# A window attention's scores and softmax weights turned and spread by DMA through DRAM

## The chip, the cores and the metric

The kernel runs on one core of one Trainium2 chip. The metric is the device time of one execution, in microseconds (us), as the median of several runs. Every engine and row below belongs to that one core.

## What is computed

A decoder of four layers over 16 sequences of 64 x 512 numbers in float32. Each layer is a cross attention followed by a feed-forward block, each with a residual. The layers are of different kinds. The change touches only the attention of the first one (layer 0), and the second layer's attention matters because its work is interleaved with it. Cut to these two:

```python
# layer 0: 64 channels, 8 heads of 8 channels, T = 512 positions, windows of 16
q = Wq @ x + bq; k = Wk @ cond + bk; v = Wv @ cond + bv      # (B, 64, 512)
k, v = pad(k, 8 left, 7 right), pad(v, 8 left, 7 right)
dots[b,h,t,w] = sum_d q[b,h,d,t] * k[b,h,d,t+w] * 8**-0.5
attn = softmax(dots, over w)                                  # 16 numbers each
out[b,h,d,t] = sum_w attn[b,h,t,w] * v[b,h,d,t+w]
x = x + Wo @ out + bo
# layer 0: an int8-quantised gated feed-forward block
# layer 1: attention with 32 query and 8 key heads of 128, RMS-normed q and k,
#          over the context's 64 rows and the latents' 64 rows
s = q @ k.T * 128**-0.5; p = softmax(s); x = x + (p @ v) @ Wo
```

So layer 0 needs, for each head and position, 16 scores, each a sum over 8 channels, and 16 weights, each of which is the same for 8 channels.

## The kernel before

**Tiles.** The activations are eight tiles x of 128 x 512 (two sequences of 64 channels each), and stay in SBUF from the first layer to the last. Layer 0 takes them in four groups of two tiles.

**Two lanes and a written order.** The program of TensorE is written out by hand: two lanes are Python generators that record instructions and yield a cost after each step, and `merged(main, side)` (line 1369) advances the side lane by the costs that the main lane has yielded, times a rate. The side lane (`first_layers`, then more) computes layer 0 for one group after another: window attention, then the int8 feed-forward block. The main lane computes layer 1's attention (`normed_attention`) for the groups that layer 0 has finished. It first makes the context's keys (line 679) and then runs its units of queries (722), keys and values (740), scores (543), softmax, turned weights (137), values (583) and output projection (592). A `Need(n, rate)` makes the main lane wait for layer 0's mark n and sets the rate from there on: 1.1 at the start, then 0.88, 0.8, 0.8 and 0.72 for the groups. After the fourth group's mark the second half of the network follows. Only TensorE's order is fixed by hand; a tile scheduler orders the other engines. Each lane has four of the eight PSUM banks.

**Layer 0's attention for a group of two tiles** (`WindowAttention`; P is 128, NH = 32 is the number of heads of two tiles, which are four sequences, and NG = 4 windows are handled at once):

1. `inputs` (lines 255 to 270): TensorE makes q, k and v, ScalarE copies them out with their bias into qs, kp and vp, the last two padded.
2. Scores: for each of four groups g of four windows and for each of the two tiles, VectorE multiplies qs with four shifted views of kp (line 293, two instructions of 128 x 1024 elements into a tile of products), and TensorE sums over the 8 channels of a head by a product with a 0/1 matrix `group` (line 300). ScalarE copies the sums into dots (line 308). There a row is a pair of window and head, and a column is a position.
3. Turn: the softmax runs over windows, which lie on partitions. In four chunks of 128 positions TensorE transposes the four blocks of dots (line 316), so that a row is a position and the 16 windows lie along a row.
4. Softmax per chunk: maximum over the windows on VectorE (324), subtraction (325), exponential on ScalarE (326), sum (328), reciprocal (329), multiplication on GpSimd (330).
5. Turn back: TensorE transposes e (the helper at line 137, result `ps_att`), ScalarE copies it into att (338).
6. Output, for each tile and each group g of four windows (`output`): four products with a 0/1 matrix `spread` (line 367) copy each head's weight to its 8 channels, one PSUM bank for each window. VectorE multiplies each bank with a shifted view of vp (377, 128 x 512). GpSimd adds the four windows: line 379 with 128 x 1024 elements, then two additions of 128 x 512 (383, or 385 and 386). At the end TensorE multiplies the sum with Wo (356, `ps_o`), and VectorE adds it to x (395). In the first group of tiles each of the four sums is multiplied with Wo by itself (n_sums is 4); in the others a single sum over all windows is (n_sums is 1).

The tiles of products have two buffers, which the scores' prod and the output's pv share; cn (the context's rows) and e share three row buffers.

**DMA.** All transfers are issued by SyncE, in program order of the scheduler. Layer 1's weights, a store of the context's keys and values (line 701) and their loads as kT and v (lines 714 to 719) go that way, too. Layer 0 uses DMA only for x, the context and its weights.

Of the kernel before, what the change touches and what calls it, by code (L numbers as in the profile page):

```python
# [8 lines left out]
F32 = mybir.dt.float32  # L9
# [4 lines left out]
AF = mybir.ActivationFunctionType  # L14
ALU = mybir.AluOpType
AX = mybir.AxisListType

P = 128
B, S, D = 16, 64, 512
NTOK = B * S  # L20
NT = NTOK // P
NC = D // P
# [7 lines left out]
def bc(ap, axis, n):  # L30

    a = ap.unsqueeze(axis)
    shape = list(a.shape)
    shape[axis] = n
    return a.to_broadcast(shape)
# [162 lines left out]
class WindowAttention:  # L198
# [6 lines left out]
    def __init__(self, es, ln, ctx_in, wt, bias):  # L205
        self.ln, self.ctx_in = ln, ctx_in
        k, nc = ln.k, ln.nc
        NH = self.NH
        pool = ln.pool(es, "l0c", 1)

        self.group = pool.tile([P, 2, NH], F32, tag="group", name="group")
        nc.gpsimd.memset(self.group, 0.0)

        self.spread = pool.tile([P, 2 * P], F32, tag="spread", name="spread")
        for i in range(2):
            nc.vector.tensor_reduce(
                self.group[:, i, 16 * i : 16 * (i + 1)],
                k.ident.rearrange("p (h d) -> p h d", d=8),
                AX.X,
                ALU.add,  # L220
            )
        for w in range(self.NG):
            rows = slice(w * NH, (w + 1) * NH)
            nc.vector.tensor_copy(
                self.spread[rows].rearrange("p (h d) -> p h d", d=8),
                bc(k.ident[rows, rows], 2, 8),
            )

        self.wbd = pool.tile([P, 4, P], F32, tag="wbd", name="wbd")
        nc.gpsimd.memset(self.wbd, 0.0)  # L230
        self.bcol = pool.tile([P, 4], F32, tag="bcol", name="bcol")
        for r in range(2):
            rows = slice(r * S, (r + 1) * S)
            nc.sync.dma_start(self.wbd[rows, :, rows], wt)
            nc.sync.dma_start(self.bcol[rows, :], bias)
# [7 lines left out]
                yield from self.output(i, t, n_sums)  # L243

    def context(self, t):
        cn = self.pool.tile([P, D], F32, tag="row", name="cn", bufs=3)
        self.ln.nc.sync.dma_start(cn, self.ctx_in[t * P : (t + 1) * P, :])
        return cn

# [20 lines left out]
        return qs, kp, vp  # L270

    def products(self, name):
        return self.pool.tile([P, self.NG, D], F32, tag="prod", name=name, bufs=2)

    def weights(self, tiles):

        ln, nc, pool = self.ln, self.ln.nc, self.pool
        WIN, NH, NG = self.WIN, self.NH, self.NG
        self.kept = []
        cns = [self.context(t) for t in tiles]  # L280
        yield 0.0
        xns = [self.normed(t) for t in tiles]
        yield 5.0
        for xn, cn in zip(xns, cns):
            self.kept.append(self.inputs(xn, cn))
            yield 3.0
        dots = pool.tile([P, WIN // NG, D], F32, tag="dots", name="dots")
        for g in range(WIN // NG):
            ps = ln.bank([P, D], "ps_dot")
            for i, (qs, kp, _) in enumerate(self.kept):  # L290
                prod = self.products("prod")
                for w in range(0, NG, 2):
                    nc.vector.tensor_tensor(  # L293
                        prod[:, w : w + 2, :],
                        bc(qs, 1, 2),
                        windows(kp, g * NG + w, 2, D),
                        ALU.mult,
                    )
                for w in range(NG):
                    nc.tensor.matmul(  # L300
                        ps[w * NH : (w + 1) * NH],
                        lhsT=self.group[:, i, :],
                        rhs=prod[:, w, :],
                        start=i == 0,
                        stop=i == 1,
                    )
                yield 3.0
            nc.scalar.copy(dots[:, g, :], ps)

        self.att = pool.tile([P, WIN // NG, D], F32, tag="att", name="att")  # L310
        es_of = {}
        for c in range(NC + 2):
            if c < NC:
                ps = ln.bank([P, WIN, NH], "ps_dotT")
                for g in range(WIN // NG):
                    nc.tensor.transpose(
                        ps[:, g * NG : (g + 1) * NG, :].rearrange("p w h -> p (w h)"),
                        dots[:, g, c * P : (c + 1) * P],
                        ln.k.ident,
                    )  # L320
                e = pool.tile([P, D], F32, tag="row", name="e", bufs=3)
                e = e.rearrange("p (w h) -> p w h", w=WIN)
                mx = ln.small.tile([P, NH], F32, tag="mx0", name="mx0")
                nc.vector.tensor_reduce(mx, ps.rearrange("p w h -> p h w"), AX.X, ALU.max)
                nc.vector.tensor_tensor(e, ps, bc(mx, 1, WIN), ALU.subtract)
                nc.scalar.activation(e, e, AF.Exp, scale=8.0**-0.5)
                sm = ln.small.tile([P, NH], F32, tag="sm0", name="sm0")
                nc.vector.tensor_reduce(sm, e.rearrange("p w h -> p h w"), AX.X, ALU.add)
                nc.vector.reciprocal(sm, sm)
                nc.gpsimd.tensor_tensor(e, e, bc(sm, 1, WIN), ALU.mult)  # L330
                es_of[c] = e
            if c <= NC:
                yield 3.0
            if c >= 2:
                ps = ln.transposed(
                    es_of[c - 2].rearrange("p w h -> p (w h)"), WIN // NG, "ps_att"
                )
                nc.scalar.copy(self.att[:, :, (c - 2) * P : (c - 1) * P], ps)
                yield 0.5

    def output(self, i, t, n_sums):

        ln, nc = self.ln, self.ln.nc
        NH, NG = self.NH, self.NG
        n_groups = self.WIN // NG
        vp = self.kept[i][2]

        po = None
        sums = []

        def project(last):
            nonlocal po
            first = po is None
            if first:
                po = ln.bank([P, D], "ps_o")
            nc.tensor.matmul(
                po, lhsT=self.wbd[:, 3, :], rhs=sums.pop(0), start=first, stop=last
            )

        acc = None  # L360
        for g in range(n_groups):
            pv = self.products("pv")
            pss = []
            for w in range(NG):
                rows = slice(w * NH, (w + 1) * NH)
                ps = ln.bank([P, D], "ps_exp")
                nc.tensor.matmul(
                    ps,
                    lhsT=self.spread[rows, i * P : (i + 1) * P],
                    rhs=self.att[rows, g, :],  # L370
                    start=True,
                    stop=True,
                )
                pss.append(ps)
            for w, ps in enumerate(pss):
                o = g * NG + w
                nc.vector.tensor_tensor(pv[:, w, :], ps, vp[:, o : o + D], ALU.mult)  # L377
            yield 2.0
            nc.gpsimd.tensor_tensor(pv[:, 0:2, :], pv[:, 0:2, :], pv[:, 2:4, :], ALU.add)  # L379
            yield 1.4  # L380
            if g % (n_groups // n_sums) == 0:
                acc = self.pool.tile([P, D], F32, tag="acc", name="acc", bufs=2)
                nc.gpsimd.tensor_tensor(acc, pv[:, 0, :], pv[:, 1, :], ALU.add)
            else:
                nc.gpsimd.tensor_tensor(acc, acc, pv[:, 0, :], ALU.add)
                nc.gpsimd.tensor_tensor(acc, acc, pv[:, 1, :], ALU.add)
            yield 1.4
            if sums:
                project(False)
            if (g + 1) % (n_groups // n_sums) == 0:  # L390
                sums.append(acc)
        yield 6.0
        project(True)
        x = ln.k.x[t]
        nc.vector.scalar_tensor_tensor(x, po, self.bcol[:, 3:4], x, ALU.add, ALU.add)
# [993 lines left out]
def decoder_kernel(ctx: ExitStack, tc: tile.TileContext, i: dict, out: bass.AP):  # L1389
# [48 lines left out]
        yield from last_layers(b, halves[0])  # L1438

    def main():  # L1440
        yield Need(0, 1.1)
        yield from normed_attention(
            a, groups, [0.88, 0.8, 0.8, 0.72], i["l1a_w"], i["l1a_kv"], i["l1a_n"]
        )
        yield Need(len(groups) + 1, 1.0)
        a.pages(ctx)
        yield from mxfp4_ffn(a, halves[1], i["l1f_w"], i["l1f_b"])
        yield from last_layers(a, halves[1])
# [86 lines left out]
```

## Time and profile before

| what | value |
| --- | --- |
| median of 3 runs (lowest, highest) | 1815.79 us (1814.68, 1816.08) |
| the profiled execution's own time | 1816.02 us |
| its span | 1813.4 us |
| TensorE clock granted, mean | 0.985 |
| TensorE busy: 0 to 220 us | 196.7 us |
| 220 to 405 | 176.7 of 185 |
| 405 to 495 | 90.0 of 90 |
| 495 to 630 | 127.6 of 135 |
| 630 to 720 | 90.0 of 90 |
| 720 to 900 | 170.0 of 180 |
| 900 to 1813 | 864.1 of 913 |
| DMA: bytes moved, mean rate | 152.19 MB, 84 GB/s |
| line 316, 64 transposes of scores | 9.7 us busy |
| `ps_att`, 64 transposes of weights | 9.4 us busy |
| line 338, 16 copies of them | 9.4 us, 603 ns each |
| line 328, 16 sums over windows, from SBUF | 16.7 us, 1052 ns each |
| line 324, 16 maxima over windows, from PSUM | 10.8 us, 679 ns each |
| line 330, 16 multiplications by GpSimd | 20.4 us, 1277 ns each |

The stretch from the last product for the scores of a group of tiles to its last product with Wo:

| group of tiles | last score product | first output product | last output product | length |
| --- | --- | --- | --- | --- |
| 1 | 44.5 | 83.07 | 153.3 | 108.8 us |
| 2 | 260.8 | 321.41 | 361.8 | 101.1 us |
| 3 | 475.5 | 547.25 | 591.8 | 116.3 us |
| 4 | 708.8 | 777.67 | 820.1 | 111.3 us |

How to read it: "busy" is the time in which an engine had an instruction in work, and a stage's busy time beside its length shows how much room is left in it. Times in the second table are counted from the start of the span. In rows of the profile, "out<-in" gives the program's names of an instruction's result and operands, then their sizes, the count, the busy time and the mean of one, and after the next bar the idle time of the engine just before these instructions, with what ended it.

### The profile page before, as it was taken

The numbers are of one execution on the slowest core, as the hardware profiler recorded it, in microseconds if no ns is written. First come the engines' busy times: TensorE is split into PE (matmuls) and PEld (weight loads), VectorE is DVE, ScalarE is ACT, GpSimd is POOL, SyncE is SP. The second block draws the span as 40 slices with busy tenths as digits, with TensorE's granted clock in tenths as the row PEclk, the third lists the DMA queues.
The fourth block names the chain that finished last, engine by engine and source line by source line (L and its number), as shares of the span: only waits on it lengthen the run. The fifth ranks groups of instructions, "written<-read, shape, count | busy, mean of one in ns | idle before, by whom it ended". The sixth has DMA issues, their size and how long they took to land.

```text
span 1813.4 us, 21657 instructions
## 1 busy us (share of the span) xinstructions
PE 1715.1 (95%) x7660; PEld 972.8 (54%) x7660; DVE 964.8 (53%) x2048; ACT 615.3 (34%) x1933; POOL 502.4 (28%) x494
## 2 busy tenths in 40 slices
PE   7999999999999999999999999999999999999996
PEld 2324355555555655556556656554666555465653
DVE  5645477566655656656695345467236433512234
ACT  2212344334433443333334345311234422223341
POOL 1443225632255321563322123211012101110011
PEclk9989999999999999999999999999999999999999
DMA  9211223223322232323443222033111100101100
GB/s 289 97 58 64 82 77 120 77 98 102 105 87 102 90 114 90 110 83 102 177 149 111 105 91 89 24 113 102 36 52 40 44 23 30 52 30 51 39 24 27
DMA packets 62266, 152.19 MB, mean 84 GB/s; under 512 B 31696, under 2 KB 40784, under 8 KB 51280
## 3 DMA queue, kind: packets, MB, share of 16 engines
q1 hardware_dynamic: 62160, 150.83, 24.5%
q8 instruction: 61, 1.00, 0.2%
q14 instruction: 45, 0.37, 0.1%
HBM read 140.32 MB, written 10.49 MB: 83 GB/s over the span
## 4 chain that ended last, share of the span: by engine, by line
PE 46%; DVE 7%; ACT 3%; POOL 3%; DMA 1%; issue 1%; SPq 0%; ACTq 0%; POOLq 0%; DVEq 0%
PE ps_wo L592 9%; PE ps_q L1226 4%; PE ps_q L722 3%; PE ps_k L1211 3%; PE ps_h L1119 3%; PE ps_o L1144 3%; PE ps_a L583 3%; PE ps_v L1179 2%; PE ps_s L543 2%; PE ps_kv L740 2%; PE ps_pT L137 2%; PE ps_o L1346 2%; PE ps_wo L1035 2%; PE ps_q L967 2%; ACT p L558 1%; PE ps_v L946 1%
## 5 line engine op out<-in xcount | busy, mean ns | idle before, releaser
L592 PE MATMUL ps_wo<-l1a_o,aT 128*128 128x512 f32 x512 | 236.2, 605 | 0.9 <-issue 0.6
L722 PE MATMUL ps_q<-l1a_w,kvT 128*128 128x512 f32 x512 | 232.6, 597 | 0.0
L567 POOL TENSOR_TENSOR p<-p,sm 128x512 f32<-128x512 f32 x96 | 106.0, 1105 | 422.7 <-DVE sm L566 399.8
L558 ACT ACTIVATE p<-ps_s,mx 128x128 f32<-128x128 f32 x384 | 135.8, 368 | 251.9 <-DVE mx L554 209.8
L119 POOL TENSOR_TENSOR r<-r,mhalf 128x5 f32<-128x5 f32 (+1 forms) x96 | 102.1, 1064 | 286.8 <-DVE r L669 282.4
L592 PEld LDWEIGHTS ps_wo<-l1a_o,aT 128*128 128x128 f32 x512 | 96.1, 193 | 122.4 <-issue 121.4
L722 PEld LDWEIGHTS ps_q<-l1a_w,kvT 128*128 128x128 f32 x512 | 93.5, 192 | 97.8 <-issue 97.7
L141 DVE TENSOR_TENSOR x<-x,ps_wo 128x512 f32<-128x512 f32 x104 | 70.7, 680 | 140.4 <-PE ps_wo L592 114.5
L740 PE MATMUL ps_kv<-l1a_w,kvT 128*128 128x256 f32 x512 | 125.6, 389 | 5.0 <-ACT qn L732 2.7
L679 PE MATMUL ps_ckv<-l1a_kv,kvT 128*64 128x512 f32 x512 | 122.7, 623 | 3.7 <-DMA l1a_kv<-in_l1a_kv 3.7
L668 DVE TENSOR_REDUCE r<-sq 128x5 f32<-128x640 f32 (+1 forms) x96 | 65.5, 682 | 110.4 <-ACT sq L748 57.1
L543 PEld LDWEIGHTS ps_s<-kT,qT 128*128 128x128 f32 (+1 forms) x768 | 97.7, 193 | 16.0 <-issue 6.6
L740 PEld LDWEIGHTS ps_kv<-l1a_w,kvT 128*128 128x128 f32 x512 | 94.2, 194 | 20.6 <-ACT qn L732 4.4
L119 POOL TENSOR_TENSOR rs<-rs,mhalf 128x1 f32<-128x1 f32 x64 | 36.7, 579 | 234.8 <-DVE rs L128 228.4
L543 PE MATMUL ps_s<-kT,qT 128*128 128x128 f32 (+1 forms) x768 | 100.8, 278 | 0.0
L553 DVE TENSOR_REDUCE mx<-ps_s 128x4 f32<-128x512 f32 x96 | 65.6, 684 | 63.7 <-PE ps_s L543 63.5
L756 DVE TENSOR_TENSOR qn<-qn,r 128x512 f32<-128x512 f32 x64 | 47.6, 743 | 90.1 <-POOL r L119 88.9
L379 POOL TENSOR_TENSOR pv<-pv 128x1024 f32<-128x1024 f32 x32 | 75.3, 2352 | 70.9 <-DVE pv L377 65.5
L293 DVE TENSOR_TENSOR prod<-qs,kp 128x1024 f32<-128x1024 f32 x64 | 80.8, 1293 | 18.4 <-ACT kp L269 15.4
L137 PE MATMUL ps_pT<-ident,p 128*128 128x128 f32 x512 | 75.3, 276 | 15.2 <-DVE pT L574 7.0
L592 PE MATMUL ps_wo<-l3a_o,aP 128*128 128x512 f32 x192 | 86.2, 598 | 2.0 <-DVE pT L574 1.0
L1226 PE MATMUL ps_q<-kvT,l3a_w 128*128 128x256 f32 x384 | 85.7, 380 | 0.0
(205 smaller groups left out, 2891.5 us busy)
## 6 DMA issues: line engine op xcount, KB each, us to landing
l1a_w<-in_l1a_w SPq DMA_DIRECT2D x32, 1536.0 KB, 6.9
l1a_o<-in_l1a_w SPq DMA_DIRECT2D x32, 1024.0 KB, 5.1
s<-ckv SPq DMA_DIRECT2D x32, 256.0 KB, 2.0
l3a_w<-in_l3a_w SPq DMA_DIRECT2D x8, 960.0 KB, 4.9
l3a_o<-in_l3a_w SPq DMA_DIRECT2D x8, 768.0 KB, 4.3
l1a_kv<-in_l1a_kv SPq DMA_DIRECT2D x4, 1024.0 KB, 6.0
kT<-s SPq DMA_DIRECT2D x64, 64.0 KB, 2.8
v<-s SPq DMA_DIRECT2D x128, 32.0 KB, 2.7
```

Of the source, the lines that this page charges most:

```text
L119: self.nc.gpsimd.tensor_tensor(out, v, self.k.mhalf[:, : v.shape[1]], ALU.pow)
L137: self.nc.tensor.transpose(ps[:, c, :], src[:, c * P : (c + 1) * P], ident)
L293: nc.vector.tensor_tensor(prod[:, w : w + 2, :], bc(qs, 1, 2), windows(kp, g * NG + w, 2, D), ALU.mult,)
L379: nc.gpsimd.tensor_tensor(pv[:, 0:2, :], pv[:, 0:2, :], pv[:, 2:4, :], ALU.add)
L543: nc.tensor.matmul(ps[:, i, :], lhsT=qT[:, i // 2, 2 * (i % 2) : 2 * (i % 2) + 2, :].rearrange("p g s -> p (g s)"), rhs=kTs[i // 2], start ...
L558: nc.scalar.activation(p[:, i, :], ps[:, i, :], AF.Exp, bias=mx[:, i : i + 1], scale=self.scale, accum_out=sm[:, i : i + 1],)
L567: nc.gpsimd.tensor_tensor(p, p, bc(sm, 2, P), ALU.mult)
L592: self.nc.tensor.matmul(ps, lhsT=a, rhs=wo[:, g, :], start=g == 0, stop=g == len(chunks) - 1)
L679: nc.tensor.matmul(ps[j * S : (j + 1) * S], lhsT=k.context(c, 2 * t + 1 - j), rhs=w_pair[hp][:, c, :], start=c == 0, stop=c == NC - 1,)
L722: nc.tensor.matmul(ps, lhsT=k.stream(c, t), rhs=w_qkv[n][0][:, c, :], start=c == 0, stop=c == NC - 1,)
L740: nc.tensor.matmul(ps, lhsT=k.stream(c, t), rhs=w_qkv[n][1][:, c, :], start=c == 0, stop=c == NC - 1,)
L1226: nc.tensor.matmul(ps[:, j], lhsT=wq[:, c, (j0 + j) * P : (j0 + j + 1) * P], rhs=k.kvT[:, c, t : t + 2, 1:3, :], start=c == 0, stop=c == N ...
```

## The change

- The matrix `spread` and its products (line 367) are gone, and so are the transposes of steps 3 and 5 and the copy at line 338.
- Each group's scores of four windows are stored to a DRAM tile as soon as ScalarE has copied them out (four stores for two tiles), and then four loads bring them back turned: a row is now a head and a quarter of the positions, and along the row lie 16 windows x 128 positions. They go back into the tile that held dots.
- The softmax runs in place on four strided slices of that tile (32 positions each). All its operands lie in SBUF, the maximum's and the subtraction's too, which came from PSUM.
- Sixteen stores, one for each window, bring the weights into a second DRAM tile.
- `load_spread` loads them with each row read 8 times over: 1 MB for each group of four windows of a tile, straight into a tile of products. Two such loads are issued ahead of the first output step, and each output step issues the one that is two further on.
- The output step's multiplication runs in place on such a tile, in two instructions of 128 x 1024 elements with both operands in SBUF, where there were four of 128 x 512 with one operand in PSUM. GpSimd's additions are the same.
- The tiles of products have three buffers, the row buffers are two.
- The rates of the two lanes are 1.15 at the start and 0.9, 0.83, 0.83, 0.72; steps without work for TensorE yield costs of their own.

Per group of two tiles that is 4 + 4 + 16 + 8 = 32 more transfers, all issued by SyncE. Line numbers after the attention's class are higher by 4 in the changed kernel.

```diff
-        self.spread = pool.tile([P, 2 * P], F32, tag="spread", name="spread")
...
-        cn = self.pool.tile([P, D], F32, tag="row", name="cn", bufs=3)
+        cn = self.pool.tile([P, D], F32, tag="row", name="cn", bufs=2)
...
-        return self.pool.tile([P, self.NG, D], F32, tag="prod", name=name, bufs=2)
+        return self.pool.tile([P, self.NG, D], F32, tag="prod", name=name, bufs=3)
...
+        NQ = P // NH
+        dram = self.dram.tile([WIN, NH, D], F32, tag="dots", name="dots_d")
         dots = pool.tile([P, WIN // NG, D], F32, tag="dots", name="dots")
...
             nc.scalar.copy(dots[:, g, :], ps)
-        self.att = pool.tile([P, WIN // NG, D], F32, tag="att", name="att")
-        es_of = {}
-        for c in range(NC + 2):
...
+            nc.sync.dma_start(
+                dram[g * NG : (g + 1) * NG].rearrange("w h n -> (w h) n"), dots[:, g, :]
+            )
+        att = dots.rearrange("p g (w n) -> p (g w) n", n=P)
+        for g in range(WIN // NG):
+            four = slice(g * NG, (g + 1) * NG)
+            nc.sync.dma_start(
+                att[:, four, :], dram[four].rearrange("w h (q n) -> (h q) w n", q=NQ)
+            )
+        yield 4.0
+        for c in range(NQ):
+            e = att[:, :, c * NH : (c + 1) * NH]
+            mx = ln.small.tile([P, NH], F32, tag="mx0", name="mx0")
+            nc.vector.tensor_reduce(mx, e.rearrange("p w n -> p n w"), AX.X, ALU.max)
+            nc.vector.tensor_tensor(e, e, bc(mx, 1, WIN), ALU.subtract)
+            nc.scalar.activation(e, e, AF.Exp, scale=8.0**-0.5)
+            sm = ln.small.tile([P, NH], F32, tag="sm0", name="sm0")
+            nc.vector.tensor_reduce(sm, e.rearrange("p w n -> p n w"), AX.X, ALU.add)
+            nc.vector.reciprocal(sm, sm)
+            nc.gpsimd.tensor_tensor(e, e, bc(sm, 1, WIN), ALU.mult)
+            yield 3.0
+        self.att = self.dram.tile([NH, WIN, D], F32, tag="att", name="att_d")
+        for w in range(WIN):
+            nc.sync.dma_start(
+                self.att[:, w, :].rearrange("h (q n) -> h q n", q=NQ), att[:, w, :]
+            )
+        self.spread = []
+        for _ in range(2):
+            self.load_spread()
+        yield 5.0
+
+    def load_spread(self):
+        n_groups = self.WIN // self.NG
+        n = len(self.spread)
+        if n == len(self.kept) * n_groups:
+            return
+        i, g = divmod(n, n_groups)
+        NH, NG = self.NH, self.NG
+        pv = self.products("pv")
+        src = self.att[i * NH // 2 : (i + 1) * NH // 2, g * NG : (g + 1) * NG, :]
+        self.ln.nc.sync.dma_start(
+            pv.rearrange("p w n -> p (w n)"), bc(src.rearrange("h w n -> h (w n)"), 1, 8)
+        )
+        self.spread.append(pv)
...
-            pv = self.products("pv")
-            pss = []
-            for w in range(NG):
-                rows = slice(w * NH, (w + 1) * NH)
-                ps = ln.bank([P, D], "ps_exp")
-                nc.tensor.matmul(
-                    ps,
-                    lhsT=self.spread[rows, i * P : (i + 1) * P],
-                    rhs=self.att[rows, g, :],
-                    start=True,
-                    stop=True,
-                )
-                pss.append(ps)
-            for w, ps in enumerate(pss):
-                o = g * NG + w
-                nc.vector.tensor_tensor(pv[:, w, :], ps, vp[:, o : o + D], ALU.mult)
+            pv = self.spread[i * n_groups + g]
+            for w in range(0, NG, 2):
+                two = pv[:, w : w + 2, :]
+                nc.vector.tensor_tensor(
+                    two, two, windows(vp, g * NG + w, 2, D), ALU.mult
+                )
+            self.load_spread()
...
-        yield Need(0, 1.1)
+        yield Need(0, 1.15)
...
-            a, groups, [0.88, 0.8, 0.8, 0.72], i["l1a_w"], i["l1a_kv"], i["l1a_n"]
+            a, groups, [0.9, 0.83, 0.83, 0.72], i["l1a_w"], i["l1a_kv"], i["l1a_n"]
```

More of the change, by code (lines that the diff above doesn't have):

```diff
@@ L221, in __init__ @@
             )
-        for w in range(self.NG):
-            rows = slice(w * NH, (w + 1) * NH)
-            nc.vector.tensor_copy(
-                self.spread[rows].rearrange("p (h d) -> p h d", d=8),
-                bc(k.ident[rows, rows], 2, 8),
-            )
+        self.dram = es.enter_context(
+            ln.tc.tile_pool(name="turned", bufs=2, space=bass.MemoryType.DRAM)
+        )
         self.wbd = pool.tile([P, 4, P], F32, tag="wbd", name="wbd")
@@ L308, in weights @@
             nc.scalar.copy(dots[:, g, :], ps)
-        self.att = pool.tile([P, WIN // NG, D], F32, tag="att", name="att")
-        es_of = {}
-        for c in range(NC + 2):
[L313 to L339, printed above, removed]
@@ L341, in output @@
     def output(self, i, t, n_sums):
         ln, nc = self.ln, self.ln.nc
-        NH, NG = self.NH, self.NG
+        NG = self.NG
         n_groups = self.WIN // NG
@@ L361, in output @@
         for g in range(n_groups):
-            pv = self.products("pv")
-            pss = []
-            for w in range(NG):
-                rows = slice(w * NH, (w + 1) * NH)
-                ps = ln.bank([P, D], "ps_exp")
-                nc.tensor.matmul(
-                    ps,
-                    lhsT=self.spread[rows, i * P : (i + 1) * P],
-                    rhs=self.att[rows, g, :],
-                    start=True,
-                    stop=True,
-                )
-                pss.append(ps)
-            for w, ps in enumerate(pss):
-                o = g * NG + w
-                nc.vector.tensor_tensor(pv[:, w, :], ps, vp[:, o : o + D], ALU.mult)
+            pv = self.spread[i * n_groups + g]
[3 more added lines that the diff above has]
+                    two, two, windows(vp, g * NG + w, 2, D), ALU.mult
+                )
+            self.load_spread()
             yield 2.0
```

## The prediction

> **What bounds the kernel now.** I read the page first (busy time by engine), then the groups of instructions, then the timelines of TensorE, VectorE, GpSimd and SyncE around the first layer, then the DMA issues.
>
> ```profile
> span 1813.4 us, 21657 instructions
> PE 1715.1 (95%) x7660; PEld 972.8 (54%) x7660; DVE 964.8 (53%) x2048; ACT 615.3 (34%) x1933; POOL 502.4 (28%) x494
> ```
>
> TensorE is busy 95% of the span and nothing else is near it, so TensorE time taken out is worth its length, as long as no wait takes its place. By stage the same view gives 90.00 of 90 us busy from 405 to 495, between two window attentions, and 127.6 of 135 from 495 to 630, inside one.
>
> ```profile
> L367 PE MATMUL ps_exp<-att,spread 32*128 32x512 f32 x256 | 47.7, 643 | 12.9 <-DVE pv L377 5.7 <-ACT att L338 4.2 <-DVE x L395 2.8
> L377 DVE TENSOR_TENSOR pv<-ps_exp,vp 128x512 f32<-128x512 f32 x128 | 80.9, 680 | 8.0 <-PE ps_exp L367 8.0
> L293 DVE TENSOR_TENSOR prod<-qs,kp 128x1024 f32<-128x1024 f32 x64 | 80.8, 1293 | 18.4 <-ACT kp L269 15.4 <-PE ps_dot L300 2.9
> L379 POOL TENSOR_TENSOR pv<-pv 128x1024 f32<-128x1024 f32 x32 | 75.3, 2352 | 70.9 <-DVE pv L377 65.5 <-DVE rs L128 5.4
> ```
>
> The spreading products (L367) go; with them 12.9 us in which TensorE waited for their buffers and inputs. L379 and its two sums stay. Time on TensorE is best read from start to next start:
>
> ```profile
> 74.09 1.14 PE L367 MATMUL ps_exp<-att,spread 32*128 32x512 f32 x8
> 75.17 0.44 PE L137 MATMUL ps_ckT<-ident,ckn 128*128 128x128 f32 x2
> ...
> 259.71 1.07 PE L300 MATMUL ps_dot<-prod,group 128*32 128x512 f32 x8
> ...
> 266.39 0.60 PE L316 MATMUL ps_dotT<-ident,dots 128*128 128x128 f32 x4
> 266.83 3.60 PE L592 MATMUL ps_wo<-l1a_o,aT 128*128 128x512 f32 x8
> ...
> 321.41 1.02 PE L356 MATMUL ps_o<-acc,wbd 128*128 128x512 f32 x2
> ...
> 360.82 1.02 PE L356 MATMUL ps_o<-acc,wbd 128*128 128x512 f32 x2
> ```
>
> The first number is the start, the second the length. Four spreading products (eight instructions, two each) take 1.08 us (74.09 to 75.17), four transposes 0.44. The stretch that decides is "last score product (L300) to second output product (L356)": here 260.8 to 361.8.
>
> ```profile
> 237.78 3.21 DVE L293 TENSOR_TENSOR prod<-qs,kp 128x1024 f32<-128x1024 f32 x2
> ```
> ```profile
> 237.81 2.09 POOL L567 TENSOR_TENSOR p<-p,sm 128x512 f32<-128x512 f32 x1 [2.93 <-DVE sm L566]
> ...
> 258.12 1.04 POOL L567 TENSOR_TENSOR p<-p,sm 128x512 f32<-128x512 f32 x1 [4.74 <-DVE sm L566]
> ```
>
> The first fence is VectorE's timeline, the second GpSimd's. Alone, two L293 take 2.36 to 2.44 us and one L567 1.04; where they meet, 3.21 and 2.09: they ran in turns. (The brackets give the idle time before and what ended it.) The new product is of L293's kind, with both inputs in SBUF.
>
> ```profile
> s<-ckv SPq DMA_DIRECT2D x32, 256.0 KB, 2.0
> l1a_o<-in_l1a_w SPq DMA_DIRECT2D x32, 1024.0 KB, 5.1
> kT<-s SPq DMA_DIRECT2D x64, 64.0 KB, 2.8
> ```
>
> These are the rows nearest to the new transfers, to landing.
>
> [...] L377 (one input in PSUM) stays at 655 to 693 ns in all 128. [...] L293's median is 1218. [...]
>
> **The change part by part.**
>
> *Removed from TensorE.* Per group of two tiles 8 sets of spreading products and 8 sets of transposes: 32 x 1.08 + 32 x 0.44 = 34.6 + 14.1 = 48.7 us, and the 12.9 us of waits: 61.6 us at most. ScalarE loses 16 copies at L338 (9.4 us busy); it is 34% busy: nothing on the path.
>
> *Where the products stand now.* In the changed program's order TensorE has between the last score product and the last output product of each group the same layer-1 steps as before. One layer-1 unit is 11.4 us (L722 3.43, L592 3.44, L740 1.73, L583 0.87, L543 0.89, turns 1.0). Counted so, the work left in the four stretches is 80.9, 81.8, 90.9 and 92.6 us: the floors. They lasted 108.8, 101.1, 116.3 and 111.3 us before. 43.6 of the 48.7 us lie inside them; the other 5 lie where TensorE is full: gain 5. The new rates only set these places.
>
> *The chain through DRAM, groups 2 to 4.* After the last score product: copy and issue 1.5, store 2.0, issue and load back 3.4 (256 KB; a like load of cn took 2.9): 6.9. Softmax: from first transpose to last weight 19.4 us before (267.0 to 286.4). The maximum is now taken from SBUF (1.05 us as L328, not 0.68; 4 x 0.37 = 1.5 more), but there is no wait for transposes: 19.1; at 26.0. Then 16 stores in a row on SyncE: one issue took 0.38 to 0.42 (kT), at start 1.12 (kvT, eight in 8.98): I take 0.42, so 6.7, and 2.0 to land: 34.7. First spread load, 1 MB: 0.5 + 5.1: 40.3. Before, the first spreading product came after 27.5. DMA engines are 27 to 31% busy there; the new 11.5 MB per group (46 MB in all) hold no one up except in this chain. Behind the waiting SP lie layer-1 loads of kT, v and weights; the third MB waits for no one and the fourth for GpSimd's first sums, and the output weights behind the fifth are due just at the output product: no cost taken.
>
> *The products.* A set was 4 x 0.68 on VectorE beside 2.35 + 1.27 + 1.27 on GpSimd; now 2 x 1.22 + 4.9 = 7.3 in turns. First half, four sets: 4 x 7.3 - 1.27 = 28, and one layer-1 unit in between (L119 1.17, L567 1.04, L756 0.69, L757 0.28, two small: 3.5), handing over 1.5: 33. Output product at 40.3 + 33 + 1 = 74.3, where before it was 62 to 73 and the floor is 55 to 62. Second half: 28 - 2.4 (first product is ready) + 5 = 31, against floors of 27.6, 31.1, 31.5: 31 to 32 with the sum. Stretches: 105, 106.5, 106.5. Gains: -3.9, +9.8, +4.8: 10.7.
>
> *First group.* Last score product at 44.5 as before; store, load at 50.8 (starting loads ahead in the queue); softmax with its turns 21; stores 8.7; MB 5.6: 86.3. First sum at 93.7, 10 us after 83.07. Each set (2.44 + 3.62, and L119's 0.7 behind it) then takes 6.8: seven sets 47.6; layer-1 key products wait some 1 to 3 us at five of them, so the last output product ends near 154, before 153.3: gain 0.
>
> *Sum.* 5 + 10.7 + 0 = 15.7 of 61.6: the rest turns into waits. 1813.4 - 15.7 = 1797.7; the profiled execution's own time, 1816.0, was 2.6 over its span and 0.2 over the median 1815.8, so 1797.7 + 2.4 = 1800.
>
> **Bounds.** Store issue: 0.33 (s) saves 1.4 us a group, 5.8 in all; 1.12 costs 11.2 a group, 45 in all: 1794 to 1845. Turns: not at all, see the second rival.
>
> **Rivals.** *The chain is longer and the kernel slower.* Place: SP, from the first of the 16 stores to the first spread load. Each us there comes four times, since all four stretches end on this chain; it decides from 15.7 / 4 = 3.9 us. For: 16 issues in a row, SP queues behind waits for TensorE and GpSimd. Against: single issues measured 0.33 to 0.43. At 8 us (issues of 0.9): 4 x 8 = 32 - 15.7 = 16 slower: 1832. *The turns cost little.* Then a set is 4.9 and the first halves end near 62; stretches 92, 95, 96 and 140 at start: gains 9 + 21 + 15 + 14 + 5 = 64: 1752. Against: the two timelines above. *Nothing moves:* chain 4 us late, 1816.
>
> **How the numbers follow.** A measurement of this kernel can tell about 0.2% (3.6 us). Forecast 0.42 (own range 1780 to 1811), longer chain 0.35, cheap turns 0.14, no change 0.09. Faster 0.56, same 0.09, slower 0.35. The range is 1762 to 1840: it cuts half of the cheap turns and the end of the longer chain.
>
> **What would show it.** L367 and the turns of scores and weights gone, TensorE busy some 66 us less but idle 50 more, at L356 and at layer-1 turns behind VectorE and GpSimd; new products with a mean over 1.22 us and spread loads near 5 us; first output product 74 us after the last score product; 105 us for the second group's stretch. Wrong if it is under 65 (turns) or over 82 (SP).

## The result, and the profile after

The changed kernel takes 1839.58 us (median of 4 runs, 1836.43 to 1841.72), the kernel before 1815.93 us in the same series. The ratio is 1.0126, with a 95% interval of 1.0099 to 1.0154: slower by 1.3%, where 1800 us was forecast. One run of e11 below (1809.65 us, at a granted clock of 0.935) was in a slower state than all the others and is left out. The profiled execution took 1841.72 us, its span is 1839.9 us, 26.5 us longer than before.

From the page of the changed kernel: busy time by engine, the new products and the first of the sums, and the new loads. In the rows PE is TensorE, PEld its weight loads, DVE VectorE, ACT ScalarE, POOL GpSimd and SPq SyncE's queue.

```profile
span 1839.9 us, 21033 instructions
PE 1670.6 (91%) x7272; PEld 959.3 (52%) x7276; DVE 992.4 (54%) x1980; ACT 604.5 (33%) x1917; POOL 531.1 (29%) x494
...
L378 DVE TENSOR_TENSOR pv<-pv,vp 128x1024 f32<-128x1024 f32 x64 | 102.0, 1616 | 40.8 <-DMA pv<-att_d 40.8
...
L383 POOL TENSOR_TENSOR pv<-pv 128x1024 f32<-128x1024 f32 x32 | 81.9, 2560 | 80.0 <-DVE pv L378 68.5 <-DVE mx L558 5.3 <-DVE r L673 3.8
...
pv<-att_d SPq DMA_DIRECT2D x32, 1024.0 KB, 8.7
```

TensorE's removed work was 66.8 us (47.7 + 9.7 + 9.4), but it is busy only 44.5 us less: by this sum the rest of its instructions became 22.3 us slower. And it is idle 169.3 us in place of 98.3. So -44.5 + 71.0 = +26.5.

The next two fences are stage tables, one row for each of the four stretches from the last score product to the last output product. After the start and end come the length and the busy time of TensorE, its weight loads, VectorE, ScalarE and GpSimd, then the granted TensorE clock, the share of the DMA engines and GB/s. First the kernel before:

```profile
44.50:153.30 108.80, 102.18 (x442) 34.02 (x438) 52.37 (x106) 24.85 (x63) 46.30 (x39) 0.95 0.22 75
260.80:361.80 101.00, 97.96 (x417) 56.56 (x418) 64.63 (x116) 38.28 (x128) 57.46 (x41) 0.98 0.26 88
475.50:591.80 116.30, 110.64 (x446) 64.08 (x446) 67.09 (x121) 41.50 (x140) 59.16 (x43) 0.97 0.27 92
708.80:820.10 111.30, 106.87 (x453) 62.64 (x454) 65.25 (x119) 40.16 (x136) 58.29 (x42) 0.98 0.28 94
```

Then the changed kernel:

```profile
45.60:158.20 112.60, 85.90 (x342) 27.29 (x342) 61.83 (x91) 22.37 (x59) 49.66 (x39) 0.89 0.64 177
...
258.10:374.20 116.10, 90.91 (x326) 56.21 (x326) 70.40 (x99) 36.56 (x127) 66.70 (x42) 0.90 0.58 162
...
485.60:611.70 126.10, 99.94 (x361) 60.50 (x358) 73.10 (x108) 39.62 (x137) 68.93 (x43) 0.91 0.59 169
...
727.90:856.40 128.50, 105.44 (x369) 65.01 (x366) 78.49 (x108) 40.38 (x142) 67.06 (x44) 0.89 0.59 168
```

In each stretch TensorE does less and takes longer. Its idle time (length less busy time) was 6.6, 3.0, 5.7 and 4.4 us, 19.7 in all, and is 26.7, 25.2, 26.2 and 23.1, 101.1 in all. The stretches are 45.9 us longer; the rest of the span is 19.4 us shorter, 9.8 of it after the last stretch.

This table splits each stretch, in us, by the timelines of TensorE, SyncE and VectorE: from the end of the last score product to the first product with vp ("chain"), from there to the first output product ("sets"), from there to the end of the last ("second half"). The names e1, e2 and e5 are those of experiments further down. Group 1 makes several output products, so its columns are cut elsewhere and only its whole length is given.

| kernel | group 1, whole | group 2: chain, sets, second half | group 3 | group 4 |
| --- | --- | --- | --- | --- |
| before | 108.8 | 29.3, 31.3, 40.4 | 33.9, 37.8, 44.6 | 32.8, 36.0, 42.4 |
| forecast | 109.5 | 40.3, 34, 31 | 40.3, 34, 32 | 40.3, 34, 32 |
| changed | 112.6 | 43.0, 33.1, 40.0 | 46.3, 41.0, 38.8 | 46.2, 37.3, 45.1 |
| e1, 4 stores | 100.2 | 33.5, 37.9, 36.8 | 34.9, 47.8, 33.0 | 36.6, 43.4, 41.7 |
| e2, sums on VectorE | 106.1 | 43.3, 26.1, 31.7 | 45.2, 31.3, 33.8 | 45.0, 31.3, 37.0 |
| e5, both | 92.4 | 33.7, 28.2, 37.1 | 34.9, 36.2, 36.9 | 35.7, 34.5, 35.5 |

**The chain.** SyncE's timeline in the second group (start, length, what it issued):

```profile
282.25 10.48 SPq L331 DMA_DIRECT2D att_d<-dots  x16
292.82 1.85 SPq L349 DMA_DIRECT2D pv<-att_d  x3
...
308.11 8.51 SPq L349 DMA_DIRECT2D pv<-att_d  x2
```

The 16 stores hold SyncE for 10.48 us, 0.66 each. The loads then go out at once, but VectorE starts on the first only at 301.08. The stage table of SyncE in these microseconds (start and end, length, TensorE clock, DMA share, GB/s):

```profile
295.00:298.00 3.00, 1.00 1.03 251
298.00:301.00 3.00, 0.98 1.00 229
301.00:304.00 3.00, 0.50 1.06 262
```

The DMA engines are full at 229 to 262 GB/s. Three 1 MB loads were issued within 2 us, and the first lands after 8.2 us. That they share the engines is only a small part of it, for the fourth load, issued at 308.11, has little beside it but the last microsecond of the third, and still needs 7.2 us (from the view of this load alone, in us):

```profile
DMA to landing us min/median/max: 7.2/7.2/7.2
```

So the loads that go out together cost the first one some 1 us. The rest over the 5.1 us of the plain 1 MB load l1a_o belongs to the spread load itself; why it is slower was not tried.

**The turns.** VectorE at the second set, and later at a unit of layer 1:

```profile
305.46 3.71 DVE L378 TENSOR_TENSOR pv<-pv,vp 128x1024 f32<-128x1024 f32 x2 [1.42 <-DMA pv<-att_d]
...
337.38 0.69 DVE L760 TENSOR_TENSOR qn<-qn,r 128x512 f32<-128x512 f32 x1 [6.00 <-POOL r L119]
```

GpSimd in the same time:

```profile
305.94 2.14 POOL L387 TENSOR_TENSOR acc<-pv 128x512 f32<-128x512 f32 x1
...
331.32 1.26 POOL L390 TENSOR_TENSOR acc<-acc,pv 128x512 f32<-128x512 f32 x1
332.54 2.34 POOL L383 TENSOR_TENSOR pv<-pv 128x1024 f32<-128x1024 f32 x1
334.96 1.26 POOL L387 TENSOR_TENSOR acc<-pv 128x512 f32<-128x512 f32 x1
336.18 1.17 POOL L119 TENSOR_TENSOR r<-r,mhalf 128x5 f32<-128x5 f32 x1
```

Two products take 2.36 us alone and one sum 1.27; where they meet, the two engines are done after 3.71, about the sum of both (3.63). That is what the prediction read in the kernel before, at one place (3.21 and 2.09 us). The other lines are one unit of layer 1: its norm factor (L119) has its input at 331.4, but stands behind three sums until 336.18 (4.8 us); VectorE's next step (L760) waits for it, 6.00 us, and behind L760 stand the next set's products, the first of them at 342.60. Here the two engines take this work in the order in which it was scheduled, so layer 1 waits for the sums and the next sums for layer 1. VectorE's waits for the norm factor in the second group's second half, in the kernel before and in the changed one (us in total, times, longest):

```profile
DVE qn L756 <- POOL r L119: 5.0, 3, 2.5
```
```profile
DVE qn L760 <- POOL r L119: 14.3, 3, 6.0
```

In groups 3 and 4 it is 6.9 and 2.6 us before, 10.1 and 8.7 in the changed kernel.

**The clock.** TensorE in the third group:

```profile
540.89 1.11 PE L137 MATMUL ps_qT<-ident,qn 128*128 128x128 f32 x4 [8.57 <-DVE qn L760]
...
548.46 3.78 PE L744 MATMUL ps_kv<-l1a_w,kvT 128*128 128x256 f32 x8 [6.24 <-ACT p L562]
...
581.17 1.89 PE L744 MATMUL ps_kv<-l1a_w,kvT 128*128 128x256 f32 x8
```

The same eight products take 3.78 us after a wait of 6.24, and 1.89 in full work. The granted clock was 0.50 in every 2 us from 540 to 552, 0.63 from 552 to 554 and 1.00 from 554 to 556; in SyncE's stage table above it is 0.50 from 301 to 304, in a wait of TensorE of 7.39 us. By the two lengths of the eight products (3.78 and 1.89), half of the busy time at a clock of 0.5 is lost: an estimate from the trace gives 25.4 us in the kernel before and 41.0 here, so the clock is some 16 of the 22.3 us. The rest stays open; records of neighbouring instructions overlap (in the prediction's view of TensorE the first starts at 74.09 and lasts 1.14, past the next one's start at 75.17), so the 22.3 are rough.

### The profile page after: what moved, and what is told of

Its sections match the earlier page's. It is cut to its first block, busy times and chain, and to the rows that moved or that the text cites. A ratio compares the mean times of both kernels' runs of the same rounds, so it can differ in the third digit from the quotient of the medians.

```text
span 1839.9 us, 21033 instructions
## 1 busy us (share of the span) xinstructions
PE 1670.6 (91%) x7272; PEld 959.3 (52%) x7276; DVE 992.4 (54%) x1980; ACT 604.5 (33%) x1917; POOL 531.1 (29%) x494
## 4 chain that ended last, share of the span: by engine, by line
PE 62%; DVE 15%; POOL 9%; DMA 5%; ACT 4%; issue 3%; SPq 3%; ACTq 0%; POOLq 0%; DVEq 0%
PE ps_wo L596 10%; PE ps_q L726 6%; PE ps_ckv L683 4%; PE ps_q L1230 4%; PE ps_kv L744 3%; PE ps_s L547 3%; PE ps_k L1215 3%; PE ps_a L587 3%; DMA pv<-att_d 3%; PE ps_h L1123 3%; PE ps_o L1148 3%; POOL pv L383 3%; PE ps_v L1183 2%; POOL r L119 2%; DVE pv L378 2%
## 5 line engine op out<-in xcount | busy, mean ns | idle before, releaser
L596 PE MATMUL ps_wo<-l1a_o,aT 128*128 128x512 f32 x512 | 231.2, 594 | 0.2 <-ACT aT L790 0.2
L119 POOL TENSOR_TENSOR r<-r,mhalf 128x5 f32<-128x5 f32 (+1 forms) x96 | 104.4, 1088 | 297.6 <-DVE r L673 290.3
L744 PE MATMUL ps_kv<-l1a_w,kvT 128*128 128x256 f32 x512 | 136.7, 415 | 16.0 <-ACT p L562 11.6
L378 DVE TENSOR_TENSOR pv<-pv,vp 128x1024 f32<-128x1024 f32 x64 | 102.0, 1616 | 40.8 <-DMA pv<-att_d 40.8
L744 PEld LDWEIGHTS ps_kv<-l1a_w,kvT 128*128 128x128 f32 x512 | 100.5, 206 | 35.2 <-ACT p L562 13.1
L760 DVE TENSOR_TENSOR qn<-qn,r 128x512 f32<-128x512 f32 x64 | 52.1, 814 | 107.2 <-POOL r L119 107.1
L383 POOL TENSOR_TENSOR pv<-pv 128x1024 f32<-128x1024 f32 x32 | 81.9, 2560 | 80.0 <-DVE pv L378 68.5
L119 POOL TENSOR_TENSOR rs<-rs,mhalf 128x1 f32<-128x1 f32 x64 | 37.9, 596 | 232.4 <-DVE rs L128 223.9
L137 PEld LDWEIGHTS ps_pT<-ident,p 128*128 128x128 f32 x512 | 62.3, 146 | 60.0 <-issue 47.6
```

The source lines that it names most:

```text
L119: self.nc.gpsimd.tensor_tensor(out, v, self.k.mhalf[:, : v.shape[1]], ALU.pow)
L137: self.nc.tensor.transpose(ps[:, c, :], src[:, c * P : (c + 1) * P], ident)
L378: nc.vector.tensor_tensor(two, two, windows(vp, g * NG + w, 2, D), ALU.mult)
L596: self.nc.tensor.matmul(ps, lhsT=a, rhs=wo[:, g, :], start=g == 0, stop=g == len(chunks) - 1)
L744: nc.tensor.matmul(ps, lhsT=k.stream(c, t), rhs=w_qkv[n][1][:, c, :], start=c == 0, stop=c == NC - 1,)
```

## The experiments

A ratio is that of the run to the kernel before on the same chip, with its 95% interval; the changed kernel's is 1.0126. Two theories went in: *turns* (theory A in the expectations: the sets of products and sums are too slow, with layer 1 in the same queues; later split into the turns themselves, A1, and the queue, A2) and *chain* (theory B: the way through DRAM is too long).

### e1: four stores in place of sixteen

```diff
-        self.att = self.dram.tile([NH, WIN, D], F32, tag="att", name="att_d")
-        for w in range(WIN):
+        self.att = self.dram.tile([WIN // NG, NH, NQ, NG, P], F32, tag="att", name="att_d")
+        for g in range(WIN // NG):
             nc.sync.dma_start(
-                self.att[:, w, :].rearrange("h (q n) -> h q n", q=NQ), att[:, w, :]
+                self.att[g].rearrange("h q w n -> (h q) w n"),
+                att[:, g * NG : (g + 1) * NG, :],
             )
```

The loads and the sets follow the new layout; their sizes and counts are the same. The stores are fewer and their pieces in DRAM are longer (2 KB in place of 512 bytes), and the run doesn't tell the two apart.

> Edit: the 16 stores of the weights become 4 (one for four windows), and each position quarter keeps its own 2 KB piece in DRAM; nothing else. Theory A (turns): the sets of products and sums decide, VectorE and GpSimd take turns on them and layer 1's small steps stand behind them in both queues. Theory B (chain): the way through DRAM is too long, above all the 16 stores, 10.5 to 11.1 us in a row on SyncE. B: 4 stores take about 2.5 us, 8 us less in each of four groups, 32 in all: 1808 us. A: the first product comes earlier in the same way, but the sets after it are as slow as before and layer 1's steps meet them earlier: 1815 to 1830.

1802.39 us, ratio 0.9929 (0.9909 to 0.995). SyncE in the second group:

```profile
266.87 1.79 SPq L331 DMA_DIRECT2D att_d<-dots  x4
268.95 1.89 SPq L350 DMA_DIRECT2D pv<-att_d  x3
```

1.79 us in place of 10.48, and the chains are 9.5 to 11.4 us shorter. That is 37 us off the whole, more than the 32 that the chain theory expected; the clock helps (0.976 granted on the mean of the profiled execution, 0.966 in the changed kernel's; TensorE is busy 6.9 us less). So the chain did cost time, and 1802 us is nearer to the chain theory's 1808 than to the 1815 to 1830 of turns. But the sets became 5 to 7 us longer in each of groups 2 to 4 (table above): over half of what the chain gives is taken back there, as the turns theory had it, and the second halves return 3 to 6 us of it.

### e2: sums on VectorE

```diff
-            nc.gpsimd.tensor_tensor(pv[:, 0:2, :], pv[:, 0:2, :], pv[:, 2:4, :], ALU.add)
+            nc.vector.tensor_tensor(pv[:, 0:2, :], pv[:, 0:2, :], pv[:, 2:4, :], ALU.add)
```

and the same for the three additions into acc.

> Edit: the sums over windows (128x1024 and two 128x512 per set) go from GpSimd to VectorE, so that no set is handed over or taken in turns. Theory A (turns): a set is 2 x 1.22 + 1.22 + 2 x 0.68 = 5.0 us on VectorE alone in place of 7.3 and more, and GpSimd is free for layer 1's steps; second halves go from 39 to 45 us back to about 31, first halves lose some 9 us each: about 1780 us. Theory B (chain through DRAM): the sets are no bound, VectorE only gets 32 x 2.6 = 83 us more work: 1835 to 1850.

1785.76 us, ratio 0.984 (0.9825 to 0.9855): 54 us off the changed kernel. The groups of products and of the first sums:

```profile
L378 DVE TENSOR_TENSOR pv<-pv,vp 128x1024 f32<-128x1024 f32 x64 | 78.0, 1229 | 38.5 <-DMA pv<-att_d 38.5
L383 DVE TENSOR_TENSOR pv<-pv 128x1024 f32<-128x1024 f32 x32 | 40.7, 1272 | 0.1
```

A product takes 1229 ns in place of 1616, near the median of L293 in the kernel before (1218 ns, both operands in SBUF too), and a sum 1272 in place of 2560. VectorE has 82 instructions more and is busy only 18 us more (1010.1 against 992.4), since its products are 24.0 us shorter (78.0 against 102.0). The chain is as it was; the sets lose 6 to 10 us and the second halves 5 to 8.3. VectorE's waits for the norm factor in the second halves are 1.7, 3.2 and 2.7 us, and 52.6 of the 54 us lie in the four stretches. The chain theory's 1835 to 1850 is out. What the run doesn't separate are the end of the turns, the end of layer 1's wait behind the sums, and that a sum is quicker on VectorE (1272 ns, where GpSimd took 2352 in the kernel before) and is not handed over.

### e3 and e4: half the change each

In e3 the turns stay on TensorE and only the spreading goes through DRAM; in e4 scores and weights are turned through DRAM, loaded back, and spread by TensorE. Both keep the changed kernel's rates.

> Edit: half the change. Scores and weights are turned by transposes on TensorE as in the kernel before (19 us more TensorE work than with the whole change, and 16 ScalarE copies); only the spreading over channels goes through DRAM, with 4 stores of 256 KB and the same eight 1 MB loads. Theory A (turns): the sets with both operands in SBUF are still there, so the second halves stay near 39 to 45 us: 1820 to 1840. Theory B (chain): one way through DRAM less and 12 stores fewer, from the last score product to the first spread load about 27.5 + 2.4 + 2 + 8 = 40 us in place of 43 to 46, and no turn's landing to wait for: 1815 to 1825.

> Edit: the other half. Scores and weights are turned by DMA through DRAM (4 stores and 4 loads each way), but the spreading is done by TensorE and the products read PSUM, as in the kernel before. Theory A (turns): with one operand in PSUM there are no turns, second halves are near 30 us again, the chain is 33 us to the first spreading product against 27.5 before: 1810 to 1820. Theory B (chain): the longer chain shows in each of four stretches, 6 to 8 us each, less the 19 us of transposes: 1820 to 1832.

e3: 1863.67 us, ratio 1.0268 (1.0252 to 1.0285), worse than both theories said. Its chains are 46.6, 46.1 and 49.6 us: the first load is issued 3.4 us after the last store (0.1 in the changed kernel) and feeds a product only 11.1 to 12.4 us later. Why these loads are so late was not tried. e4: 1812.9 us, ratio 0.9987 (0.9972 to 1.0002), no change: 4 stores and 4 loads go through DRAM, the chain of 31.7 to 35.1 us is hardly longer than before, the products read PSUM, GpSimd's first sum takes 2350 ns, and the second halves are near those of before (41.0, 43.9, 46.6). The turns theory had e4's time right, but not the 30 us that it gave the second halves. So the loss is in the spreading's half, where the products with both operands in SBUF are, though in e3 its late loads add to it.

### e5: both repairs

e1's stores and e2's sums together.

> Edit: the 4 stores and the sums on VectorE together. The two alone took 37 and 54 us off the changed kernel. If they are two terms of one sum (the chain before the first product, the sets after it), they add up until TensorE's own work in the stretches is reached: first halves 60 to 67 us against floors of 54 to 62, so 1750 to 1762 us. If they are the same wait seen twice (TensorE then stands for layer 1's steps instead), the pair gives little over the better one: 1775 to 1786.

1758.68 us, ratio 0.9686 (0.9647 to 0.9724). 81 us off the changed kernel, where the two alone gave 37 and 54: in the main two terms of one sum. Where the other 10 us went was not tried. The stage table of TensorE alone (length, busy, clock, DMA share, GB/s):

```profile
46.10:138.40 92.30, 83.23 (x342) 0.94 0.77 215
...
238.30:337.40 99.10, 87.53 (x329) 0.95 0.72 190
...
448.80:556.70 107.90, 96.47 (x361) 0.95 0.74 196
...
672.90:778.60 105.70, 97.03 (x369) 0.98 0.73 204
```

Idle time in the stretches is 41 us in place of 101. TensorE is busy for 1649.1 us, 66.0 less than in the kernel before: the removed work all but in full, and next to nothing for a slower clock (20.7 us by the estimate above, 25.4 in the kernel before). This is the fastest version that computes the whole, 3.1% faster than the kernel before.

### e6 and e13: layer 1's steps off GpSimd, in both kernels

```diff
-        nc.gpsimd.tensor_tensor(p, p, bc(sm, 2, P), ALU.mult)
+        nc.vector.tensor_tensor(p, p, bc(sm, 2, P), ALU.mult)
...
-            ln.rsqrt(r, r)
+            nc.vector.reciprocal(r, r)
```

The second edit leaves the inverse root out. The first is in a function that the last layer's attention uses too; in the kernel before, the time after layer 1 is the same without the edit and with it (611.0 and 611.4 us).

> Edit: the changed kernel with its sums on GpSimd as they are, but layer 1's two GpSimd steps in a unit go to VectorE: the multiplication by the softmax's reciprocal sum (0.69 us there), and in place of the inverse root a reciprocal (0.2 us; so layer 1's norm factors are not the reference's). Theory A1 (turns): product and sums exclude each other, so a set stays 7.3 us and over: at most 15 us better than the changed kernel, 1825 to 1840. Theory A2 (queue): the sets cost because layer 1's GpSimd steps stand behind 4.9 to 7 us of sums and VectorE and TensorE behind them: most of the 54 us that the sums on VectorE gave: 1785 to 1800.

> Edit: e6's edit in the kernel before (layer 1's multiplication to VectorE, a reciprocal there in place of the inverse root, so its norm factors are not the reference's). Theory A2 (queue behind sums, where TensorE has no other work): the kernel before has 19.7 us of idle TensorE in its four stretches, so at most 20 us better: 1795 to 1812. If shorter layer-1 steps are a gain of their own, the 45 us of e6 show here too: 1765 to 1780.

e6: 1794.96 us, ratio 0.9893 (0.9858 to 0.9929), 45 us off the changed kernel, as A2 said. But e13: 1777.79 us, ratio 0.9782 (0.9758 to 0.9806): the same edit takes 39 us off the kernel before, where no sum takes turns with a product (all 128 at L377 take 655 to 693 ns). So most of e6's gain is one that these steps give anywhere, and A2 as the only cause falls. By the ratios, the changed kernel is 1.26% behind the kernel before with these steps on GpSimd, and 1.13% (0.9893 / 0.9782) without, about the same. In the four stretches alone the edit takes 31.5 us off the changed kernel and 18.2 off the kernel before: some 13 us there may be the queue's, and in e6 the second halves (34.7, 37.9 and 40.1 us) are still longer than in e2.

### e7: sums on VectorE in the kernel before

> Edit: the kernel before, with only its sums over windows moved from GpSimd to VectorE. TensorE is idle for only 3 to 6.6 us in each of its four stretches, 19.7 us in all, and its products read PSUM and take no turns. Theory A1 (turns): no gain, 1812 to 1825, VectorE only gets 83 us more work. Theory A2 (queue): GpSimd's sums hold layer 1's steps here too, up to 12 us better: 1803 to 1812.

1804.67 us against 1814.96, ratio 0.9936 (0.9919 to 0.9953): 10 us off, in A2's band, and A1's "no gain" was wrong. Yet the same edit gave 54 us in the changed kernel, and the other 44 come with the change. Turns are part of them: a product lost 387 ns there (1616 against 1229), 24.8 us of VectorE's time over 64, and in the kernel before, with its sums on GpSimd, all 128 products stay at 655 to 693 ns. Some 13 may be the queue's (e6 and e13). And a rival stands: in the kernel before TensorE is busy for 94 to 97% of the stretches, so quicker sums could show little there even without any turn. No run puts GpSimd's sums beside products that read PSUM where TensorE has room.

### e8, e9 and e12: the rates

The rates of the changed kernel in the kernel before (e8), those of before in the changed kernel (e9) and in e5 (e12).

> Edit: the kernel before, with only the two lanes' rates of the changed kernel (1.15 and 0.9, 0.83, 0.83, 0.72). The rates only place layer 1's steps in TensorE's order: 1810 to 1822 by every theory; more than that would mean that the placing is a cause of its own.

> Edit: the changed kernel with the kernel before's rates (1.1 and 0.88, 0.8, 0.8, 0.72). The new rates alone made the kernel before 30 us slower, all of it after the fourth group, though all theories had said no change. Theory C (placing): the new rates are at fault in the changed kernel too, and without them it is some 20 to 30 us faster: 1810 to 1820. Theory A2 with the chain: the changed kernel's longer yields need the higher rates (side cost per group about 147 to 151, rates 2 to 4 percent higher), so they cancel in it, and the old ones leave it as slow or slower: 1835 to 1855.

> Edit: e5 (4 stores, sums on VectorE) with the kernel before's rates. In the changed kernel they took 16.5 us off, all after the fourth group, where one unit of layer 1 less was left. If the placing is a term of its own, it comes off here too: 1740 to 1750. If the rates only paid for the long chain and suit the shorter one: 1755 to 1775.

e8: 1845.29 us, ratio 1.0159 (1.0122 to 1.0196), a miss for every theory. e9: 1823.13 us, ratio 1.0055 (1.0037 to 1.0072), 16.5 us off the changed kernel (13 by the ratios), near theory C (the placing). So with the old rates the change is 0.55% behind the kernel before, not 1.26%. e12: 1761.86 us, ratio 0.9699 (0.9672 to 0.9725), no gain over e5. The next two fences show the time after the last stretch, with the busy time of layer 1's query products in it (eight instructions are one unit), first in the changed kernel, then in e9.

```profile
856.40:1840.00 983.60, 75.62 (x168) 30.39 (x168) 0.99 0.20 68
```
```profile
857.30:1823.00 965.70, 72.13 (x160) 28.94 (x160) 0.99 0.20 68
```

The last stretch ends at the same time in both (856.4 and 857.3); e9 has one unit of layer 1 less to do after it, 20 in place of 21, and that part is 17.9 us shorter. In e8 it holds 23 units and lasts 1018.6 us, against 22 and 993.3 in the kernel before. In e12 that part is 14 us shorter than in e5, with 20 units against 21, and the stretches are 10 longer. So the new rates alone cost 30 us in the kernel before, 16.5 in the changed one and nothing in e5, and most of that is units of layer 1 left for the part after the last stretch. Why a unit there is worth 14 to 25 us, where 11.4 of TensorE's time were counted for one, was not settled.

### e10 and e11: more than e5

e10 has larger costs for the chain's steps (8, 4.5 and 10) and rates 10% higher; e11 has layer 1's multiplication by the reciprocal sum on VectorE.

> Edit: 4 stores and sums on VectorE as in e5, and the chain's steps yield more (4, 3 and 5 become 8, 4.5 and 10, 15 more for a group), with rates 10 percent higher to keep the sum: some layer-1 steps move from between the stretches into the wait for DRAM. In e5 TensorE is idle 41 us in the four stretches and 17 between them. If the wait is only badly filled: up to 20 us off, 1738 to 1752. If layer 1's steps in it wait for VectorE anyway, or are missed between the stretches or after the fourth group: 1755 to 1775.

> Edit: e5, and layer 1's multiplication by the reciprocal sum goes from GpSimd (1.04 us and two handovers) to VectorE (0.69 us). By A2 what is left of the queue on GpSimd is now only this and the inverse root, and neither stands behind sums any more: little to gain, 1752 to 1760; a gain of over 8 us would say that the handovers between the two engines themselves are a bound.

e10: 1795.42 us, ratio 0.9898 (0.987 to 0.9927), 37 us worse than e5 and worse than both readings said. Second halves are 5 to 6 us shorter (30.9, 32.0, 29.4), but the sets take 42.3, 50.4 and 46.8 us: one more unit of layer 1 stands among them (over the span TensorE waits 13.8 us for VectorE before the scores of L556, 7.0 in e5). The wait for DRAM can't be filled with layer 1 in this way. e11: 1762.09 us, ratio 0.9722 (0.9702 to 0.9741), no gain over e5.

## Why the prediction was wrong

It forecast 15.7 us of gain and came to 26.5 us of loss. The points below overlap in part and are not to be added up:

- **Removed work: right, with a term missing.** 66.8 us of busy time went. But the instructions left became 22.3 us slower, some 16 of it, by the estimate above, at a granted clock of 0.5, and no step of the working had it: "TensorE busy some 66 us less but idle 50 more" became 44.5 less and 71.0 more. In e5, with 41 us of idle time in the stretches in place of 101, the term is nil.
- **The chain: mechanism right, size off.** 40.3 us were forecast to the first spread load, 43.0, 46.3 and 46.2 measured in groups 2 to 4. The 16 stores took 10.5 to 11.1 us, where 6.7 and 2.0 to land were counted; the price of one issue was taken from a 64 KB load (0.42 us), and these are 0.66. The first load took 8.2 to 8.4 us, where 0.5 + 5.1 were counted: the row that it came from was one of plain loads, and a spread load takes 7.2 us with hardly anything beside it; the prefetch that follows it adds 1. The softmax came as forecast (19.1; for group 2 the stores start 24.1 us after the last score product, against 26.0).
- **The sets: the price of a turn right, layer 1's share wrong.** The products do take turns with the sums (3.71 us where they meet, 3.63 for the two alone), and the second group's first four sets took 33.1 us, where 34 was forecast. The failed step is "Second half: 28 - 2.4 (first product is ready) + 5 = 31", whose 5 is the first half's price of one unit (3.5 + 1.5), and in the first half "one layer-1 unit in between". GpSimd's timeline has three units' norm factors (L119) in each second half and one or two among the first sets, each in the sets' own queues, and in the second halves VectorE stood 14.3, 10.1 and 8.7 us for them. Second halves came to 40.0, 38.8 and 45.1, no better than before, and these three are 29 us of the 56 us by which the four stretches missed the forecast; the chain is 15 of them (groups 2 to 4), the first sets 9, and group 1 3. With the sums on VectorE (e2) the same second halves take 31.7, 33.8 and 37.0, near the forecast of 31 to 32, with as much of layer 1 in them.
- **One group stood for three.** First output products 76.1, 87.3 and 83.4 us after the last score product, where 74.3 was forecast for all: the second group was worked out and copied. The table of the kernel before had 60.6, 71.8 and 68.9 for the same three. Groups 3 and 4 passed the 82 us that were to speak for SyncE; e1 bears that out in part, but their first sets are 3 to 7 us of it.
- **The rates: priced at nothing, wrongly.** "The new rates only set these places" left out what the places are worth: 16.5 us in this kernel (e9), over half of the loss.
- **Outside the stretches** a gain of 5 us was forecast and 19.4 measured, 9.8 of it after the last stretch, where one unit of layer 1 less was left (21 in place of 22).
- **The rivals.** The longer chain (1832 us, place SyncE, decisive from 3.9 us a group) has the right sign, and e1 shows its place: 8.7 us less on SyncE is worth 37 us. But the chain was 3 to 6 us over the forecast and not 8, and e2 shows a larger term beside it. Cheap turns (1752 us) are refuted by the products' 1616 ns; e5 comes to 1759 us, without the turns (1233 ns a product) and with a shorter chain.

What stays open: how the 44 us of e2 over e7 divide among turns, queue and quicker sums, why a spread load is slower than a plain one, the lateness of e3's loads, and how to price a place in the lanes' order beforehand.

## What to carry to other kernels

When a product's second operand moves from PSUM to SBUF, look at what GpSimd does with the result: here sums that had run beside it (655 to 693 ns for each product that read PSUM) then ran in turns with it (1616 ns for a product of twice the size, 1229 with no sum on GpSimd), and moving them to VectorE was worth more than the whole change (54 us, against 10 where PSUM was read). A way through DRAM is priced by issues and landings of transfers of the same shape, not by those of plain ones (a spread load took 7.2 us with little beside it, a plain one 5.1), and a wait of TensorE can cost more than its length: after the 6.24 us above the next eight products took 3.78 us, where 1.89 was their time in full work. Where two lanes share engines, work out every stretch by itself, with all that stands in the queues, and try the order's rates apart from the rest.

## What the runs showed that was not expected

- Sixteen stores of 64 KB hold SyncE for 10.5 to 11.1 us; the same megabyte in four stores of 256 KB, in longer pieces, for 1.8 us.
- A 1 MB load that reads each row 8 times over lands after 7.2 us with hardly anything beside it, a plain one after 5.1.
- The new rates of two interleaved lanes alone made the kernel before 1.6% slower, and without them the changed one is 0.7% faster.
- Two GpSimd steps per layer-1 unit (1.04 and 1.17 us, GpSimd busy for 28% of the span) were worth 39 us of the kernel before (e13, which leaves the inverse root out), though TensorE is busy 95% of the time there; the busy shares don't show it.
